# Attention of a macaron block, batch by batch: where values and late scores stand in TensorE's order

## The chip, the cores and the metric

The kernel runs on one core of a Trainium2 chip. The metric is the device time of one execution in microseconds (us), lower is better. TensorE is called PE here, VectorE DVE, ScalarE ACT, GpSimd POOL and SyncE SP, as in the profile.

## What is computed

Sixteen sequences of 256 tokens with 256 channels go through a block of three parts: half a feed-forward, an attention, half a feed-forward, all float32, with a layer norm ahead of each. Each feed-forward has 32 routed experts (4 per token) and a shared one. The attention has 16 query heads and 8 key heads of 32 channels, rotary positions, a soft cap, and a causal mask:

```python
x = x + 0.5 * ffn(layernorm(x))
x = x + attention(layernorm(x))
x = x + 0.5 * ffn(layernorm(x))

# attention, b a sequence, h a query head
att = einsum('bhqd,bhkd->bhqk', q, k) * scale
att = 50.0 * tanh(att / 50.0)
att = where(causal, att, -inf)
y = einsum('bhqk,bhkd->bhqd', softmax(att), v)
```

## The kernel before

**Stages.** The 32 tiles of 128 tokens form eight groups (`NG`) of four tiles, that is of two batches (sequences). The first feed-forward runs first, then the attention over all groups, then the second feed-forward. Work of the shared expert is cut into steps (L382 `shared`: six steps of gate products `pg`, four of output products `po`), which `Fill` hands out wherever PE would otherwise wait: `EXPERT_FILL` says how many us of it stand beside each expert, `SPARE` how many beside the units of the attention. `fill` is the shared expert of the first feed-forward, `fill2` that of the second.

**Order.** PE's order is written by hand throughout. From L734 on that holds for DVE, ACT and POOL too: each of these runs its instructions in the order in which the Python code issues them. Several activities are generators that are advanced by a step now and then, so that their instructions stand between those of others:

- `project(pool, g)` (L478) makes queries, keys and values of group g: reads the sums of the experts (a DMA on SP), adds them on POOL, takes the statistics (`moments`, four pairs of bn_stats and bn_aggr on DVE), normalises on ACT, transposes (`pta`), then eight pieces of products, six `pq` and two `pv`. For a `pq` piece, `turned` (L509) has a shuffle and a product on DVE and a product and a sum on POOL behind two matmuls.
- `route(1, g, rows)` (L232) prepares the second feed-forward's routing of group g: `moments`, then `xr` (four scalings on DVE, L250), two pairs of transposes `pt` with their copies on ACT, the logits `pl` on PE with four copies and reductions on DVE, an Exp on ACT, and a tail of some fourteen small DVE instructions (L299 to L316) ahead of a DMA to `xtab`.

In the loop of the attention `mine` is the projection of the group behind the present one, `ahead` that of the group behind that.

**A unit of the attention.** A unit is a group, one of its two batches and one of two chunks m of four key heads (eight query heads). `scores` (L549) treats the unit's two key tiles one after the other: the first against all 256 queries (matmuls `sc` of 512 columns), the second against the later 128 (256 columns). Each of four matmuls uses 32 rows of the array, `lhsT=kT[r, m, ...]` with `r` one of four strips of 32 partitions, and writes a PSUM bank of its own. Two PSUM tiles of two banks, `big` with two buffers, hold them; `pg` uses the same two buffers. Tanh and Exp follow on ACT, half by half (L568, L571), and POOL cuts the diagonal (L573).

`values` (L586) has five or so groups of four matmuls, each of which writes 32 of the 128 output rows: the softmax's denominators `den`, by a product with ones, and the sums `y`. Its last group is a product of ones with `plate`, which `late_sums` (L580) has DVE add from both key tiles' later queries; units without it sum the wider tile instead. Then DVE turns and inverts the denominators and scales (L610 to L617). `project_out` (L620, `poa`) ends a batch.

**The loop before** (L778) goes over units k. It issues `late_sums` of unit k-1, the first key tile's scores of unit k, `poa` of a finished batch, pieces of `mine` (by `PROJECT_PIECES`), the second key tile's scores of unit k, the values of unit k-1, then steps of routing, spare work and projection. Most value groups thus come right behind the narrow scores.

Of the kernel before, what the change touches and what calls it, by code (L numbers as in the profile page):

```python
# [9 lines left out]
F32 = mybir.dt.float32  # L10
BF16 = mybir.dt.bfloat16
I32 = mybir.dt.int32
AF = mybir.ActivationFunctionType
# [27 lines left out]

ROUTE_FILL, SLOT_FILL, FIRST_FILL, EXPERT_FILL, SUM_FILL, PROJECT_FILL = 3.0, 1.7, 6.0, (2.15, 2.3), 17.0, 1.5
LAST_FILL = 8.0
MASK_FILL, ROW_FILL = 4.0, 3.2
WARM = (9, 3)
AHEAD = 3
SPARE = (0.0, 0.0, 2.0, 3.0)
LAST = 4 * (NG - 1)  # L50
PROJECT_PIECES = ((2, 1), (0, 2), (2, 1), (0, 0))


_COLS = {}
# [39 lines left out]
def macaron_kernel(ctx: ExitStack, tc: tile.TileContext, X, Wq, Wk, Wv, Wo, w_norm, w_router, w_gate, w_up,  # L94
# [451 lines left out]
                    )  # L546
                    yield 1.75

    def scores(pool, u, qT, kT):  # L549

        _, b, m = u
        t0 = b * T
        made = []
        for k0, w in ((0, T), (P, P)):
            dst = pool.tile([P, 4, 2, w], F32, name=f"p{w}", bufs=2)
            sc = [big.tile([P, 2, 2 * T], F32, tag="big", name="sc") for _ in range(2)]
            for i in range(4):
                r = slice(HD * i, HD * (i + 1))  # L560
                nc.tensor.matmul(  # L561
                    sc[i // 2][:, i % 2, 0 : 2 * w].rearrange("p (s t) -> p s t", s=2),
                    lhsT=kT[r, m, t0 + k0 : t0 + k0 + P], rhs=qT[r, m, :, t0 + T - w : t0 + T],
                    start=True, stop=True,
                )
            parts = [dst[:, 2 * h : 2 * h + 2].rearrange("p j s t -> p j (s t)") for h in range(2)]
            for h in range(2):
                nc.scalar.activation(parts[h], sc[h][:, :, 0 : 2 * w], AF.Tanh, scale=QK_SCALE / SOFTCAP)  # L568
            for h in range(2):

                nc.scalar.activation(parts[h], parts[h], AF.Exp, scale=SOFTCAP)  # L571
                diag = dst[:, 2 * h : 2 * h + 2, :, 0:P].rearrange("p j s t -> p (j s) t")
                nc.gpsimd.affine_select(  # L573
                    out=diag, in_=diag, compare_op=ALU.is_ge, fill=0.0,
                    base=0, pattern=[[0, 4], [1, P]], channel_multiplier=-1,
                )
            made.append(dst)
            yield made

    def late_sums(pool, pa, pb):  # L580

        dst = pool.tile([P, 4, 2, P], F32, name="plate", bufs=1)
        nc.vector.tensor_add(dst, pa[:, :, :, P:T], pb)
        return dst

    def values(pool, u, v, pa, pb, pc, yT):  # L586

        _, b, m = u  # L590
        y = ps1.tile([P, 2, T], F32, tag="aux", name="y")
        den = ps1.tile([P, 2, T], F32, tag="aux", name="den")
        late = slice(P, T)
        va, vb = [[v[:, 2 * b + j, 4 * m + i, :] for i in range(4)] for j in range(2)]
        products = [
            (y, slice(0, T), va, pa, True, False),
            (y, late, vb, pb, False, True),
        ]
        if pc is None:
            products = [(den, slice(0, T), [ones] * 4, pa, True, False)] + products  # L600
            products += [(den, late, [ones] * 4, pb, False, True)]
        else:
            products = [(den, slice(0, P), [ones] * 4, pa[:, :, :, 0:P], True, True)] + products
            products += [(den, late, [ones] * 4, pc, True, True)]
        for dst, at, w, p, start, stop in products:
            for i in range(4):
                nc.tensor.matmul(dst[HD * i : HD * (i + 1), :, at], lhsT=w[i], rhs=p[:, i], start=start, stop=stop)  # L607
# [12 lines left out]
    def project_out(g, b, yT):  # L620
        for qh in range(2):
            t = g * GT + 2 * b + qh
            po = ps1.tile([P, C], F32, tag="mm", name="poa")
            for c in range(4):
                nc.tensor.matmul(  # L625
                    po, lhsT=yT[:, c // 2, c % 2, qh * P : (qh + 1) * P], rhs=wo[:, c // 2, c % 2, :],
                    start=(c == 0), stop=(c == 3),
                )
            nc.vector.tensor_add(x[:, t, :], po, x[:, t, :])
# [138 lines left out]
            late.append(i)  # L768

    fill2 = Fill(sh, end)  # L770
    units = [(g, b, m) for g in range(NG) for b in range(2) for m in range(2)]
    with tc.tile_pool(name="attn", bufs=1, reuse_waits="tile") as pool:
        probs, outs, routing = {}, {}, {}

        def spare_time(us):
            (fill if fill.done < NG else fill2).take(us)

        for k in range(len(units) + 2):  # L778
            g, j = divmod(k, 4)
            u = units[k] if k < len(units) else None  # L780
            mine, ahead = projects.get(g + 1), projects.get(g + 2)

            def unit_values():
                if 1 <= k <= len(units):
                    d = units[k - 1]
                    if d[2] == 0:
                        outs[d[:2]] = pool.tile([P, 2, 2, T], F32, name="yT")
                    values(pool, d, made[d[0]][2], *probs.pop(d), outs[d[:2]])

            if 1 <= k <= len(units):
                d = units[k - 1]
                probs[d].append(late_sums(pool, *probs[d]) if 1 < k <= LAST else None)
            if u:
                parts = scores(pool, u, *made[g][:2])
                next(parts)
            if k >= 2 and units[k - 2][2] == 1:
                d = units[k - 2][:2]
                project_out(*d, outs.pop(d))  # L800

            before, behind = PROJECT_PIECES[j] if k != 1 else PROJECT_PIECES[j][::-1]
            advance(mine, before)
            if k == LAST:
                fill2.step()
            if mine is None and j % 2 == 0:
                unit_values()
            if u:
                probs[u] = next(parts)

            if j == 0:
                advance(routing.get(g - 2))
            if j == 2:
                advance(routing.get(g - 2))
            if mine is not None or j % 2:
                unit_values()


            if j == 3 and k > LAST:
                advance(routing.get(g - 1))  # L820
                advance(routing.get(g - 2))
            if j == 3 and k < LAST:
                advance(ahead)

            if k == LAST - 2:
                fill2.gates()
            elif k == LAST + 4:
                fill2.step()
            elif LAST - 2 < k < LAST + 3:
                if k != LAST + 1:  # L830
                    fill2.step()
            elif not LAST - 5 <= k < LAST - 2:
                spare_time(SPARE[j])
            if j == 3 and k < LAST:
                advance(routing.get(g - 1))
                advance(routing.get(g - 2))
            advance(mine, behind)
            if j == 1 and g >= 1:
                routing[g - 1] = route(1, g - 1, rows)
                next(routing[g - 1])  # L840
                advance(routing.get(g - 2))
                fill2.ready = max(g - 1, 0)
            if j == 2:
                advance(routing.get(g - 1))
                advance(ahead)
            if j == 0:
                advance(routing.get(g - 2))

            fill.finish(min(g + 3, NG))
            if j == 3:  # L850
                advance(ahead)
            elif j < 2:
                advance(ahead)
            if j == 3 and g + 3 < NG:
                projects[g + 3] = project(pp, g + 3)
                next(projects[g + 3])
# [45 lines left out]
```

## Time and profile before

| | |
|---|---|
| median of 3 runs | 1051.61 us (1050.84 to 1052.44) |
| the profiled execution | 1051.13 us |
| its span, first to last instruction | 1049.4 us |
| mean granted PE clock over the span | 0.999 |
| PE busy from 800 to 1020 us (second experts) | 215.32 of 220 us |
| DVE busy in the attention, 378 to 755 us | 283.99 of 377 us |
| ACT busy there | 243.88 us |
| POOL busy there | 256.92 us |

A row of the groups reads: line, engine, operation, output and inputs, shapes, count, busy us and mean ns of one. A float32 matmul stands as two passes in the trace, so `x8` of scores are four matmuls. A row of the timeline reads: start in us, length in us, the same names, count, and in brackets the engine's idle time before it and who ended that. Since matmuls overlap at their ends, a group's own cost is read from its start to the start of the next. A row of windows reads: the window, its length, busy us (and instructions) of PE, PE's weight loads, DVE, ACT and POOL, the granted PE clock, the DMA engines' share and GB/s.

### The profile page before, as it was taken

The numbers are of one execution on the slowest core, as the hardware profiler recorded it, in microseconds if no ns is written. First come the engines' busy times: TensorE is split into PE (matmuls) and PEld (weight loads), VectorE is DVE, ScalarE is ACT, GpSimd is POOL, SyncE is SP. The second block draws the span as 40 slices with busy tenths as digits, with TensorE's granted clock in tenths as the row PEclk, the third lists the DMA queues.
The fourth block names the chain that finished last, engine by engine and source line by source line (L and its number), as shares of the span: only waits on it lengthen the run. The fifth ranks groups of instructions, "written<-read, shape, count | busy, mean of one in ns | idle before, by whom it ended". The sixth has DMA issues, their size and how long they took to land.

```text
span 1049.4 us, 15591 instructions
## 1 busy us (share of the span) xinstructions
PE 1024.0 (98%) x5432; PEld 647.1 (62%) x5432; DVE 631.7 (60%) x1684; ACT 400.0 (38%) x761; POOL 495.9 (47%) x548
## 2 busy tenths in 40 slices
PE   9999999999999999999999999999999999999998
PEld 5656656876866455545555555555566576867665
DVE  4964674445353446787878869775756644454453
ACT  3442111222221247675757567667310122222201
POOL 4410102455553379688677767753100245555441
PEclk9999999999999999999999999999999999999999
DMA  9731802788872100000101010000300167777563
GB/s 286 213 120 46 248 6 59 166 167 171 174 164 33 45 22 1 21 21 1 44 1 44 2 43 4 20 23 2 108 23 1 34 133 168 169 167 160 100 202 133
DMA packets 137869, 92.97 MB, mean 89 GB/s; under 512 B 80512, under 2 KB 135104, under 8 KB 137792
## 3 DMA queue, kind: packets, MB, share of 16 engines
q1 hardware_dynamic: 125504, 74.16, 25.6%
q0 software_dynamic: 12288, 17.83, 10.1%
q8 instruction: 43, 0.70, 0.3%
q14 instruction: 34, 0.28, 0.1%
HBM read 60.99 MB, written 30.97 MB: 88 GB/s over the span
## 4 chain that ended last, share of the span: by engine, by line
PE 84%; DVE 7%; POOL 2%; issue 2%; DMA 2%; ACT 1%; POOLq 0%; DVEq 0%; ACTq 0%
PE pg L399 24%; PE po L411 14%; PE pge L446 8%; PE pq L512 7%; PE poe L459 5%; PE poa L625 5%; PE sc L561 5%; PE y L607 3%; PE den L607 3%; PE pv L540 3%; PE pl L283 2%; PE pte L438 1%; DVE xr L250 1%; DVE st L221 1%; PE pa L369 1%
## 5 line engine op out<-in xcount | busy, mean ns | idle before, releaser
L399 PE MATMUL pg<-xnT,sw 128*128 128x512 f32 x704 | 318.5, 597 | 2.0 <-DVE act L405 2.0
L399 PEld LDWEIGHTS pg<-xnT,sw 128*128 128x128 f32 x704 | 130.0, 190 | 138.3 <-issue 130.2
L462 POOL DMA_INDIRECT acc<-y,idx x64 | 101.4, 1584 | 183.8 <-DVE y L461 65.4
L411 PE MATMUL po<-swd,act 128*128 128x256 f32 x768 | 179.3, 383 | 3.9 <-DVE x L415 1.3
L403 ACT ACTIVATE act<-pg 128x512 f32<-128x512 f32 x96 | 57.2, 596 | 288.3 <-PE pg L399 280.5
L411 PEld LDWEIGHTS po<-swd,act 128*128 128x128 f32 x768 | 142.9, 190 | 35.0 <-issue 9.8
L404 DVE SCALAR_TENSOR_TENSOR act<-act,pg 128x512 f32<-128x512 f32 x96 | 65.7, 684 | 152.4 <-ACT act L403 131.1
L568 ACT ACTIVATE p<-sc 128x512 f32<-128x512 f32 (+1 forms) x128 | 97.0, 809 | 81.6 <-PE sc L561 81.2
L422 POOL DMA_INDIRECT xg<-xtab,idx x64 | 68.0, 1062 | 75.4 <-DVE idx L377 56.5
L446 PE MATMUL pge<-xgT,wgu 128*112 128x128 f32 (+1 forms) x768 | 95.9, 275 | 7.7 <-issue 5.7
L571 ACT ACTIVATE p<-p 128x512 f32<-128x512 f32 (+1 forms) x128 | 101.0, 845 | 0.0
L573 POOL TENSOR_SCALAR_AFFINE_SELECT p<-p 128x512 f32<-128x512 f32 x128 | 82.6, 673 | 37.5 <-ACT p L571 36.0
L446 PEld LDWEIGHTS pge<-xgT,wgu 128*112 128x112 f32 (+1 forms) x768 | 88.6, 182 | 11.4 <-issue 11.4
L415 DVE SCALAR_TENSOR_TENSOR x<-po,sg,x 128x256 f32<-128x256 f32 x64 | 30.9, 482 | 72.4 <-PE po L411 70.7
L441 ACT ACTIVATE xgT<-pte,wnorm 128x128 f32<-128x128 f32 x128 | 39.9, 365 | 74.7 <-PE pte L438 65.4
L405 DVE TENSOR_TENSOR act<-act,pg 128x512 f32<-128x512 f32 x96 | 65.7, 684 | 2.3
L459 PE MATMUL poe<-wd,sie 112*128 112x256 f32 x256 | 65.9, 379 | 0.1
L520 POOL TENSOR_TENSOR qs<-qs,kc 128x512 f32<-128x512 f32 x48 | 61.5, 1281 | 9.2 <-DVE qs L515 9.2
L561 PE MATMUL sc<-qT,kT 32*128 32x256 f32 (+1 forms) x512 | 63.5, 533 | 0.4 <-DVE act L405 0.4
L512 PE MATMUL pq<-hT,wq 128*128 128x512 f32 x128 | 60.9, 599 | 0.0
L625 PE MATMUL poa<-wo,yT 128*128 128x256 f32 x256 | 59.7, 386 | 1.2 <-DVE qT L519 1.2
L452 DVE SCALAR_TENSOR_TENSOR sie<-sie,pge 112x256 f32<-112x256 f32 x64 | 26.9, 420 | 53.1 <-ACT sie L451 40.9
(109 smaller groups left out, 1362.1 us busy)
## 6 DMA issues: line engine op xcount, KB each, us to landing
xtab<-xr SPq DMA_DIRECT2D x16, 576.0 KB
acc<-zero SPq DMA_DIRECT2D x2, 4224.0 KB
a<-acc SPq DMA_DIRECT2D x16, 512.0 KB
wgu<-in_L_ffn_w_gate SPq DMA_DIRECT2D x64, 112.0 KB
wgu<-in_L_ffn_w_up SPq DMA_DIRECT2D x64, 112.0 KB
wd<-in_L_ffn_w_down SPq DMA_DIRECT2D x64, 112.0 KB
wgu<-in_L_ffn_w_gate SPq DMA_DIRECT2D x64, 64.0 KB
wgu<-in_L_ffn_w_up SPq DMA_DIRECT2D x64, 64.0 KB
```

What stands on the lines that cost most here:

```text
L399: nc.tensor.matmul(pg[:, s, :], lhsT=sw[:, c, w0 : w0 + P], rhs=xnT[:, c, cols], start=(c == 0), stop=(c == 1))
L411: nc.tensor.matmul(po, lhsT=act[:, k, t * P : (t + 1) * P], rhs=swd[:, k, :], start=(k == 0), stop=(k == len(FC) - 1),)
L422: nc.gpsimd.indirect_dma_start(out=xg, out_offset=None, in_=xtab[n], in_offset=bass.IndirectOffsetOnAxis(ap=idx[:, e : e + 1], axis=0), bo ...
L446: nc.tensor.matmul(pg[:fw, n_, :], lhsT=wgu[:, c, w0 : w0 + fw], rhs=xgT[:, c, :], start=(c == 0), stop=(c == 1))
L459: nc.tensor.matmul(po, lhsT=si[:, k, :], rhs=wd[:, k, :], start=(k == 0), stop=(k == 1))
L462: nc.gpsimd.indirect_dma_start(out=acc[n], out_offset=bass.IndirectOffsetOnAxis(ap=idx[:, e : e + 1], axis=0), in_=y, in_offset=None, boun ...
L512: nc.tensor.matmul(pq, lhsT=weights[:, c, :], rhs=hT[:, c, :], start=(c == 0), stop=(c == 1))
L561: nc.tensor.matmul(sc[i // 2][:, i % 2, 0 : 2 * w].rearrange("p (s t) -> p s t", s=2), lhsT=kT[r, m, t0 + k0 : t0 + k0 + P], rhs=qT[r, m, ...
L568: nc.scalar.activation(parts[h], sc[h][:, :, 0 : 2 * w], AF.Tanh, scale=QK_SCALE / SOFTCAP)
L571: nc.scalar.activation(parts[h], parts[h], AF.Exp, scale=SOFTCAP)
L573: nc.gpsimd.affine_select(out=diag, in_=diag, compare_op=ALU.is_ge, fill=0.0, base=0, pattern=[[0, 4], [1, P]], channel_multiplier=-1,)
L625: nc.tensor.matmul(po, lhsT=yT[:, c // 2, c % 2, qh * P : (qh + 1) * P], rhs=wo[:, c // 2, c % 2, :], start=(c == 0), stop=(c == 3),)
```

## The change

The loop goes over batches instead of units. Each step n has two halves, one for each chunk: `late_sums` and values of batch n-1's chunk, then at once the first key tile's scores of batch n's chunk, then a piece of projection (`between`). The second key tile's scores of both chunks are made together, in one block of eight matmuls whose two chunks share PSUM banks, and one pair of Tanh, Exp and diagonal cut each. Routing, spare work and projection are put at new places around these, and two amounts of fill change. `late_sums` is left out for six units in place of five.

```diff
-ROUTE_FILL, SLOT_FILL, FIRST_FILL, EXPERT_FILL, SUM_FILL, PROJECT_FILL = 3.0, 1.7, 6.0, (2.15, 2.3), 17.0, 1.5
+ROUTE_FILL, SLOT_FILL, FIRST_FILL, EXPERT_FILL, SUM_FILL, PROJECT_FILL = 3.0, 1.7, 6.0, (2.05, 2.3), 17.0, 1.5
...
-SPARE = (0.0, 0.0, 2.0, 3.0)
-LAST = 4 * (NG - 1)
-PROJECT_PIECES = ((2, 1), (0, 2), (2, 1), (0, 0))
+
+SPARE, FIRST_SPARE, LAST_SPARE = 4.0, 2.6, 6.0
...
+    def exponentials(dst, sc):
...
+        parts = [dst[:, 2 * h : 2 * h + 2] for h in range(2)]
+        flat = [p.rearrange("p i m s t -> p i (m s t)") for p in parts]
+        for h in range(2):
+            nc.scalar.activation(flat[h], sc[h], AF.Tanh, scale=QK_SCALE / SOFTCAP)
+        for h in range(2):
+
+            nc.scalar.activation(flat[h], flat[h], AF.Exp, scale=SOFTCAP)
+            diag = parts[h][..., 0:P].rearrange("p i m s t -> p (i m s) t")
+            nc.gpsimd.affine_select(
...
+    def scores(pool, b, chunks, qT, kT, k0):
...
+        t0, w = b * T, T - k0
+        dst = pool.tile([P, 4, len(chunks), 2, w], F32, name=f"p{w}", bufs=3 - len(chunks))
+        sc = [big.tile([P, 2, 2 * T], F32, tag="big", name="sc") for _ in range(2)]
+        for n_, m in enumerate(chunks):
             for i in range(4):
                 r = slice(HD * i, HD * (i + 1))
                 nc.tensor.matmul(
...
+                    sc[i // 2][:, i % 2, n_ * 2 * w : (n_ + 1) * 2 * w].rearrange("p (s t) -> p s t", s=2),
+                    lhsT=kT[r, m, t0 + k0 : t0 + k0 + P], rhs=qT[r, m, :, t0 + k0 : t0 + T],
                     start=True, stop=True,
                 )
...
+        exponentials(dst, sc)
+        return [dst[:, :, n_] for n_ in range(len(chunks))]
...
+        for n in range(2 * NG + 1):
+            g, b = divmod(n, 2)
+            past = divmod(n - 1, 2)
             mine, ahead = projects.get(g + 1), projects.get(g + 2)
...
+            def between():
+
+                if mine is None:
+                    fill2.step()
+                else:
+                    advance(mine)
+
+            def unit_values(m):
+                if n:
+                    if m == 0:
+                        outs[past] = pool.tile([P, 2, 2, T], F32, name="yT")
+                    pa, pb = early.pop((*past, m)), later[past][m]
+
+                    pc = late_sums(pool, pa, pb) if 1 < n < 2 * NG - 1 else None
+                    values(pool, (*past, m), made[past[0]][2], pa, pb, pc, outs[past])
+
+
+
+            unit_values(0)
+            if g < NG:
+                early[g, b, 0] = scores(pool, b, [0], *made[g][:2], 0)[0]
+            between()
+
+            if b == 0:
                 advance(routing.get(g - 2))
+            else:
+                advance(ahead)
+            unit_values(1)
+            if g < NG:
+                early[g, b, 1] = scores(pool, b, [1], *made[g][:2], 0)[0]
+            if n < 2 * NG - 1:
+                between()
+            if b == 0:
+                advance(ahead)
+            else:
+                advance(routing.get(g - 1))
+            if n == 0:
+                advance(mine, 2)
+            elif g < NG:
+                project_out(*past, outs.pop(past))
+            if g < NG:
+                later[g, b] = scores(pool, b, [0, 1], *made[g][:2], P)
+            if b == 0:
                 advance(routing.get(g - 2))
+                advance(mine, 1 if n == 0 else 2)
+                if g < 2:
+                    spare_time(FIRST_SPARE)
+                elif g == NG - 1:
+                    fill2.step()
+                elif g == NG:
+                    fill2.step()
+                    project_out(*past, outs.pop(past))
+                advance(routing.get(g - 2))
+                advance(ahead)
+                if g >= 1:
+                    routing[g - 1] = route(1, g - 1, rows)
+                    next(routing[g - 1])
+                    fill2.ready = max(g - 1, 0)
+            else:
+                advance(routing.get(g - 2))
                 advance(routing.get(g - 1))
+                advance(mine, 2)
+                if g < NG - 2:
+                    spare_time(FIRST_SPARE if g == 0 else SPARE)
+                elif g == NG - 2:
+                    fill2.gates()
+                else:
+                    fill2.take(LAST_SPARE)
+                advance(ahead, 2)
                 advance(routing.get(g - 2))
...
+                if g + 3 < NG:
+                    projects[g + 3] = project(pp, g + 3)
+                    next(projects[g + 3])
             fill.finish(min(g + 3, NG))
```

More of the change, by code (lines that the diff above doesn't have):

```diff
@@ L547, in project @@
                     yield 1.75
[L549 to L558, printed above, removed]
+    def exponentials(dst, sc):
[7 more added lines that the diff above has]
+            nc.gpsimd.affine_select(
+                out=diag, in_=diag, compare_op=ALU.is_ge, fill=0.0,
+                base=0, pattern=[[0, diag.shape[1]], [1, P]], channel_multiplier=-1,
+            )
+    def scores(pool, b, chunks, qT, kT, k0):
[3 more added lines that the diff above has]
+        for n_, m in enumerate(chunks):
             for i in range(4):
@@ L561, in scores @@
                 nc.tensor.matmul(
-                    sc[i // 2][:, i % 2, 0 : 2 * w].rearrange("p (s t) -> p s t", s=2),
-                    lhsT=kT[r, m, t0 + k0 : t0 + k0 + P], rhs=qT[r, m, :, t0 + T - w : t0 + T],
+                    sc[i // 2][:, i % 2, n_ * 2 * w : (n_ + 1) * 2 * w].rearrange("p (s t) -> p s t", s=2),
+                    lhsT=kT[r, m, t0 + k0 : t0 + k0 + P], rhs=qT[r, m, :, t0 + k0 : t0 + T],
                     start=True, stop=True,
                 )
[L566 to L578, printed above, removed]
+        exponentials(dst, sc)
+        return [dst[:, :, n_] for n_ in range(len(chunks))]
     def late_sums(pool, pa, pb):
@@ L770, in macaron_kernel @@
     fill2 = Fill(sh, end)
-    units = [(g, b, m) for g in range(NG) for b in range(2) for m in range(2)]
     with tc.tile_pool(name="attn", bufs=1, reuse_waits="tile") as pool:
-        probs, outs, routing = {}, {}, {}
+        early, later, outs, routing = {}, {}, {}, {}
         def spare_time(us):
             (fill if fill.done < NG else fill2).take(us)
-        for k in range(len(units) + 2):
-            g, j = divmod(k, 4)
-            u = units[k] if k < len(units) else None
+        for n in range(2 * NG + 1):
+            g, b = divmod(n, 2)
+            past = divmod(n - 1, 2)
@@ L781, in macaron_kernel @@
             mine, ahead = projects.get(g + 1), projects.get(g + 2)
[L783 to L809, printed above, removed]
@@ L811, in macaron_kernel @@
-            if j == 0:
-                advance(routing.get(g - 2))
-            if j == 2:
-                advance(routing.get(g - 2))
-            if mine is not None or j % 2:
-                unit_values()
-            if j == 3 and k > LAST:
-                advance(routing.get(g - 1))
-                advance(routing.get(g - 2))
[L822 to L847, printed above, removed]
@@ L849, in macaron_kernel @@
-            fill.finish(min(g + 3, NG))
[L850 to L856, printed above, removed]
+            def between():
[10 more added lines that the diff above has]
+                    values(pool, (*past, m), made[past[0]][2], pa, pb, pc, outs[past])
```

## The prediction

> **What bounds the kernel now.** First the busy shares, then the stretch of the attention (378 to 755 us), then who makes TensorE wait there.
>
> ```profile
> PE 1024.0 (98%) x5432; PEld 647.1 (62%) x5432; DVE 631.7 (60%) x1684; ACT 400.0 (38%) x761; POOL 495.9 (47%) x548
> ```
> ```profile
> 378.00:755.00 377.00, 372.56 (x2443) 201.50 (x2441) 283.99 (x667) 243.88 (x374) 256.92 (x313) 1.00 0.07 22
> ```
> ```profile
> PE poa L625 <- DVE qT L519: 1.2, 1, 1.2
> PE den L607 <- DVE plate L583: 0.9, 2, 0.6
> ```
>
> TensorE (PE) has work for 372.6 of 377 us at the full clock, with hardly any DMA, and waits a few us in all. So a us less of PE's stream is a us of the end, and so is a us in which PE waits. What is in the stream besides arithmetic stands in the starts of PE's groups:
>
> ```profile
> 485.58 1.98 PE L512 MATMUL pq<-hT,wk 128*128 128x512 f32 x4
> 487.40 1.88 PE L512 MATMUL pq<-hT,wq 128*128 128x512 f32 x4
> 489.21 0.71 PE L561 MATMUL sc<-qT,kT 32*128 32x256 f32 x8
> 489.86 0.64 PE L607 MATMUL den<-p,ones 128*32 128x256 f32 x8
> 490.31 1.47 PE L607 MATMUL y<-p,v 128*32 128x512 f32 x16
> 491.60 0.61 PE L607 MATMUL den<-plate,ones 128*32 128x256 f32 x8
> 492.15 3.70 PE L399 MATMUL pg<-xnT,sw 128*128 128x512 f32 x8
> ```
>
> Read from start to start. A 512-wide pass streams in 0.43 us, a 256-wide one in 0.216. Scores (S, 32-row tiles) and values (V, 32-column tiles) run four at a time, so eight 256-wide score matmuls should take 0.43; they take 0.65. The difference sits at each change of the array's shape: about 0.10 on the last instruction before it and 0.10 on the first after it (0.02 where V begins). With F for full-size work: F to S 0.20, S to F 0.21, S to V 0.13, V to S 0.22, V to F 0.22, F to V 0.12.
>
> **Part 1, fewer changes of shape.** I counted them in the order of the built programs, attention alone. Before: 61, 34, 30, 3, 29, 2 in the sequence above, 30.4 us. After: 18, 48, 0, 30, 2, 32, 24.4 us. Joining the two chunks in one block assumes that the second pair of passes costs only its streaming; the row-tiled `pa` passes of the slots stage, several of which follow each other, show only the first of them longer (0.215 against 0.111). One more unit goes without late sums, and its wide sum of ones costs 0.4. Gain 5.6.
>
> **Part 2, waits that go.** Six score blocks of before ran in two halves, as a PSUM pair was not free (the page's waits on DVE act at scores, 0.4 us, are part of it): 1.54 or 2.4 in place of 1.07, together 4.6. With the 0.9 on plate and 1.2 on poa shown, 6.7; none of it has to vanish, so 0 to 6.7. A value block of 2.2 us now stands ahead of the first scores, which gives the pairs their time, so I take 6.7.
>
> **Part 3, the wait that comes.** The value block needs `plate`, the sum that VectorE makes in `late_sums`, for its last product. Before, `late_sums` stood at the start of a unit and a score block, a `poa` or `pq` and another score block lay between. Now it is issued just ahead of the value block, which reaches plate after 0.43+0.02+0.86+0.43 = 1.74 us. VectorE works strictly in program order (its trace has the order of the build). This is before, with the step of routing and the statistics ahead of plate:
>
> ```profile
> 533.84 0.42 DVE L221 BATCH_NORM_STATS2 st<-x 128x6 f32<-128x256 f32 x1
> ...
> 535.97 0.26 DVE L287 COPY lg<-pl 128x132 f32<-128x132 f32 x1
> ...
> 536.87 0.42 DVE L221 BATCH_NORM_STATS2 st<-x 128x6 f32<-128x256 f32 x1
> ...
> 539.00 1.19 DVE L583 TENSOR_TENSOR plate<-p,p 128x1024 f32<-128x1024 f32 x1
> 540.12 0.01 DVE L515 LOAD_MASK_SELECT qs<-pq  x1
> ```
>
> From 533.84 to 540.12, 6.28 us: four statistics 2.13, the four copies and reductions of logits 0.90, four more statistics 2.13, plate 1.12. PE reached its den of plate at 541.92: hidden.
>
> The new loop's step n issues the scores of batch n and the values of batch n-1, in two value blocks. First block, odd n. The build has on PE pl, then the values at once; and VectorE: the four logit steps, which wait for pl, all eight statistics, plate. The copy starts about 0.13 after the value block does; plate is there at 0.13+6.28+0.06 = 6.47, PE wants it at 1.74: 4.7 us. Four steps so (5, 7, 9, 11); step 3 has no logits (4.4), step 13 four statistics (2.6). Sum 25.8.
>
> First block, even n. On PE pg, two pta (0.98 with the shape), values; on VectorE the two steps of that pg, the tail of routing, plate:
>
> ```profile
> 606.73 0.69 DVE L404 SCALAR_TENSOR_TENSOR act<-act,pg 128x512 f32<-128x512 f32 x1 [2.15 <-ACT act L403]
> 607.45 0.69 DVE L405 TENSOR_TENSOR act<-act,pg 128x512 f32<-128x512 f32 x1
> 608.05 0.28 DVE L299 TENSOR_REDUCE tot<-ex 128x4 f32<-128x128 f32 x1
> ...
> 610.86 1.21 DVE L583 TENSOR_TENSOR plate<-p,p 128x1024 f32<-128x1024 f32 x1
> ```
>
> Counted from the end of pg: ScalarE's Tanh and two VectorE steps 2.24, tail 2.81, plate 1.2: 6.3, wanted at 0.98+1.74 = 2.7. That is 3.55 for n = 6, 8, 10, 12; step 14 has no pta and waits 4.45; step 4 has no pg and waits 0.3. Sum 19.0.
>
> Second block. Behind the first one VectorE turns the sums (L610 to L615, 2.48, begun 0.68 after the last product starts), then serves the pq between (1.24) and only then adds plate: 6.05 against PE's 5.28, so 0.77 in six even steps; with a pv between (copy 0.61) about 0.17 in six odd ones. Sum 5.6.
>
> ScalarE: the merged block puts two Tanh and two Exp of 1024 (4.2) ahead of the copies of pt (0.94), and pl needs these 4.0 after the block's end: 5.2 against 4.0, 1.2 five times, 6.2. VectorE again: `xr` (four, 4.1 with GpSimd busy beside it) precedes the adds of poa, so pt's PSUM tile is late by 0.7 to 1.3 in six odd steps, 5.4. Step 16 has pg and a tail between its two value blocks, 2.0.
>
> All waits 25.8+19.0+5.6+6.2+5.4+2.0 = 64.0. Behind a waiting value product on PE stands everything else, the next scores first, so nothing covers these. The merging saves ScalarE some 12 us of fixed cost and leaves POOL's selected elements as they are, neither on the path. Steps of routing and projection that move take their DMAs on SP along: xtab is written and acc read some us later or earlier, with 7% of the DMA engines busy; zero. EXPERT_FILL moves 34 x 0.1 = 3.4 us of PE's fill from the experts to later, the same PE work: 0, or 0.4 for one more uncovered expert.
>
> **The clock.** No wait of before is long enough to show what a 4.7 us gap does to TensorE, except the last:
>
> ```profile
> 1040.00:1049.00 9.00, 5.80 (x27) 4.75 (x26) 2.72 (x6) 0.00 (x0) 0.00 (x0) 0.95 0.16 54
> ```
>
> PE's last matmul ends at 1045.8; a mean clock of 0.95 over 9 us is 0.9 us at half clock, so it fell about 2.35 us after the last matmul. The Trainium skill (TensorE: Matmul & The Clock Gate, "What's actually happening") puts it at a full free-running idle window of some 3.4 us, and the same time of work to come back. By the row, some eight of the waits above (all the long odd ones, two thirds of the 3.55 ones) drop the clock; by the page about two (a 4.7 us gap holds a whole window in 4 of 10 cases). Coming back took the first matmuls from 1.19 to 6.9 us at half speed; in a busy stretch I estimate 2.5 us lost each (a window and a half at half speed, from the page's length). Eight give 20, two 5. I take the five gaps well over both bounds, 12.5, less 1 of the small waits it hides: 11.5.
>
> Sum: 1051.1 - 5.6 - 6.7 + 64.0 + 11.5 = 1114.3 against the profiled execution; the median of the runs is 0.5 above that, so 1115.
>
> **Rivals.** (a) The shape changes decide: if plate were ready within 1.74 us at every value block, PE's stream would only get shorter, 1051.6 - 5.6 - 6.7 = 1039, or 1045 if only the shapes give. It needs new waits of under 12 us in total; for it speaks that the work of PE is what counts and is cut for certain, against it that the 6.28 us chain is measured and stands in the build behind pl. (b) Only the chain behind pl binds: the tails run in slack of their own, as VectorE is ahead there, and the clock holds. Without 19.0 and 11.5, 1084. For it: the tail's inputs are early; against: it is queued behind pg's two steps. (c) The clock drops in eight waits, 8.5 more, and ScalarE or POOL is late for the merged block by up to 1 us in each of 15 steps: up to 1138. That the build doesn't place values beside scores can be excluded; it has 30 such neighbours in place of 3.
>
> **Chances.** Forecast 0.60, (b) 0.17, (c) 0.13, (a) 0.07, a cancelling mixture around no change 0.03. About 0.2% is what a measurement here tells from no change. The range 1072 to 1138 covers the forecast with its bounds, (b) and most of (c).
>
> **What would show it.** In the profile after: PE waiting on DVE plate for 40 to 55 us, the longest waits in odd steps near 4.7, others on ACT xnT at pl; a granted clock under 1 within the attention; 16 merged score blocks, each 1.07 from start to start. If plate waits total under 10 us, the reasoning about VectorE's order is wrong; if they are as said and the clock stays 1, the time is about 1103.

## The result, and the profile after

The changed kernel takes 1153.26 us (median of 6 runs, 1151.33 to 1160.0) against 1051.69 before (6 runs): a ratio of 1.0964, 95% interval 1.0942 to 1.0986. The forecast of 1115 had the sign right and the size too small: +63 in place of +101.6, with the time outside the range.

From the profile after, the busy shares and the granted clock over the span:

```profile
PE 1049.1 (91%) x5432; PEld 653.5 (57%) x5432; DVE 622.8 (54%) x1683; ACT 391.2 (34%) x697; POOL 491.5 (43%) x516
...
PEclk9999999999999999989899999998999999999989
```

PE has the same 5432 matmuls. It lost seven points of its share, and the clock, nearly full before, dips from the middle on. The attention, and two neighbouring stretches of 10 us inside it:

```profile
382.50:835.50 453.00, 382.28 (x2389) 198.92 (x2392) 264.46 (x619) 231.87 (x302) 245.72 (x270) 0.94 0.05 16
562.00:572.00 10.00, 5.39 (x30) 2.34 (x23) 7.11 (x20) 1.83 (x3) 5.55 (x11) 0.66 0.00 0
572.00:582.00 10.00, 9.73 (x68) 5.28 (x67) 7.86 (x13) 7.78 (x11) 4.01 (x5) 1.00 0.01 2
```

The first row is the whole stage: 453 us, PE idle for 71 of them, at a clock of 0.94. The second row is a value block that waits for plate: half idle, the clock at 0.66, while the row after it is full. So the loss comes in single places. Who makes PE wait, whole kernel:

```profile
PE den L609 <- DVE plate L585: 49.5, 18, 4.6
PE pq L511 <- DVE qT L518: 8.4, 6, 1.4
PE pv L539 <- DVE qT L518: 7.5, 5, 1.5
...
PE po L410 <- DVE x L414: 5.0, 3, 4.4
```

A row gives the idle time in total, the number of waits and the longest. The first row was 0.9 us before and the last 1.3; the two between are new. Inside one step (n = 7) PE's timeline shows the wait, and DVE's shows what it is made of:

```profile
560.49 0.64 PE L609 MATMUL den<-p,ones 128*32 128x256 f32 x8
560.95 1.47 PE L609 MATMUL y<-p,v 128*32 128x512 f32 x16
567.03 1.08 PE L609 MATMUL den<-plate,ones 128*32 128x256 f32 x8 [4.61 <-DVE plate L585]
```
```profile
560.60 0.30 DVE L286 COPY lg<-pl 128x132 f32<-128x132 f32 x1 [1.01 <-PE pl L282]
...
561.53 0.42 DVE L220 BATCH_NORM_STATS2 st<-x 128x6 f32<-128x256 f32 x1
...
565.78 1.19 DVE L585 TENSOR_TENSOR plate<-p,p 128x1024 f32<-128x1024 f32 x1
```

DVE begins the logits 0.11 us after PE begins the value block, works without a pause through logits and eight statistics (561.53 to 565.78) and only then adds plate; PE reads it 6.54 us after the block began. Before, the same chain of 6.28 us ran under score and projection work. The matmuls on plate show 1.08 in place of 0.64: they ran at half clock.

**Where the 101 us are.** I summed PE from start to start of its passes, each against what its width streams, and put each excess down to a wait, to a change of shape or to half clock. (A wait counted so is some 0.2 us longer than the idle time in a row of the profile.) Between the two profiled executions (1051.13 and 1152.32):

| us | before | after |
|---|---|---|
| attention: streaming | 321.8 | 329.1 |
| attention: waits | 4.6 | 78.2 |
| attention: half clock | 0 | 21.8 |
| attention: changes of shape | 28.3 | 23.3 |
| all other stages: streaming | 663.4 | 654.0 |
| all other stages: waits | 24.7 | 34.2 |
| all other stages: half clock | 0 | 4.4 |
| all other stages: changes of shape | 1.4 | 0.3 |

The clock rows can be had in a second way: the trace has 61.4 us at half clock, 8.6 of them in gaps where PE has nothing to lose; half of the rest is 26.4.

For the waits and the clock of the other stages the forecast had no term. Some 9.4 us of the shared expert's matmuls stand in the attention now (44.7 in place of 35.3) and not around it: 2.5 came from ahead of the attention and 6.8 from behind the last routed expert. Yet the stages around it did not get shorter. At the kernel's end that is plain:

```profile
1111.68 5.49 PE L410 MATMUL po<-swd,act 128*128 128x256 f32 x12 [4.36 <-DVE x L414]
```

PE waits 4.36 us for DVE's `x`, which stands in DVE's queue behind an addition (L767) that waits 8.14 us for the read-back of the experts' sums. There are 40.8 us of shared-expert work after the last routed expert in place of 47.7; the end takes 53.1 us in place of 52.7.

### The profile page after: what moved, and what is told of

The parts are those of the page before. It is cut to its first block, busy times and chain, and to the rows that moved or that the text cites. A ratio compares the mean times of both kernels' runs of the same rounds, so it can differ in the third digit from the quotient of the medians.

```text
span 1150.6 us, 15482 instructions
## 1 busy us (share of the span) xinstructions
PE 1049.1 (91%) x5432; PEld 653.5 (57%) x5432; DVE 622.8 (54%) x1683; ACT 391.2 (34%) x697; POOL 491.5 (43%) x516
## 4 chain that ended last, share of the span: by engine, by line
PE 77%; DVE 15%; issue 2%; ACT 2%; DMA 2%; POOL 2%; DVEq 0%; POOLq 0%; ACTq 0%
PE pg L398 24%; PE po L410 12%; PE pq L511 8%; PE pge L445 7%; PE sc L574 5%; PE poa L627 5%; PE poe L458 4%; DVE plate L585 3%; PE pv L539 3%; PE den L609 2%; PE pl L282 2%; DVE st L220 2%; DVE act L403 1%; DVE qs L514 1%; PE pte L437 1%
## 5 line engine op out<-in xcount | busy, mean ns | idle before, releaser
L410 PE MATMUL po<-swd,act 128*128 128x256 f32 x768 | 184.0, 391 | 10.0 <-DVE x L414 5.0
L410 PEld LDWEIGHTS po<-swd,act 128*128 128x128 f32 x768 | 146.3, 195 | 42.1 <-issue 11.9
L554 ACT ACTIVATE p<-sc 128x1024 f32<-128x1024 f32 x96 | 93.0, 1021 | 186.0 <-PE sc L574 179.6
L559 POOL TENSOR_SCALAR_AFFINE_SELECT p<-p 128x512 f32<-128x512 f32 (+1 forms) x96 | 80.3, 845 | 155.5 <-ACT p L557 137.7
L557 ACT ACTIVATE p<-p 128x1024 f32<-128x1024 f32 x96 | 96.2, 1058 | 0.0
L445 PEld LDWEIGHTS pge<-xgT,wgu 128*112 128x112 f32 (+1 forms) x768 | 88.6, 182 | 10.6 <-issue 10.6
L519 POOL TENSOR_TENSOR qs<-qs,kc 128x512 f32<-128x512 f32 x48 | 64.9, 1353 | 12.5 <-DVE qs L514 12.5
L511 PE MATMUL pq<-hT,wq 128*128 128x512 f32 x128 | 61.4, 606 | 8.4 <-DVE qT L518 8.4
L609 PE MATMUL den<-plate,ones 128*32 128x256 f32 x208 | 18.8, 438 | 50.0 <-DVE plate L585 49.5
```

What stands on the lines that cost most here:

```text
L410: nc.tensor.matmul(po, lhsT=act[:, k, t * P : (t + 1) * P], rhs=swd[:, k, :], start=(k == 0), stop=(k == len(FC) - 1),)
L445: nc.tensor.matmul(pg[:fw, n_, :], lhsT=wgu[:, c, w0 : w0 + fw], rhs=xgT[:, c, :], start=(c == 0), stop=(c == 1))
L511: nc.tensor.matmul(pq, lhsT=weights[:, c, :], rhs=hT[:, c, :], start=(c == 0), stop=(c == 1))
L554: nc.scalar.activation(flat[h], sc[h], AF.Tanh, scale=QK_SCALE / SOFTCAP)
L557: nc.scalar.activation(flat[h], flat[h], AF.Exp, scale=SOFTCAP)
L559: nc.gpsimd.affine_select(out=diag, in_=diag, compare_op=ALU.is_ge, fill=0.0, base=0, pattern=[[0, diag.shape[1]], [1, P]], channel_multip ...
```

## Experiments

The theory: DVE's order makes plate late, and each long wait also costs clock. The rivals: the merged score block on ACT is the main cause; late issue of the sum is enough by itself; or the changed neighbours on PE are worth nothing at all. Runs e1 to e8 and e11 are one execution each. The six of the changed kernel spread over 8.7 us, so a difference of a few us between two of them says little.

**e1: no unit has late sums.** All 32 units take the wider product of ones; plate is not made.

```diff
-                    pc = late_sums(pool, pa, pb) if 1 < n < 2 * NG - 1 else None
+                    pc = None
```

> The changed kernel without late sums at all: every value block takes its denominators from the two key tiles directly, which costs PE 0.43 us in each of 26 units, 11 us. Theory O (VectorE's program order ahead of plate makes PE wait, and the waits drop the clock): the 54 us of waits on plate go and most of the 26 us of half clock with them, 1152 - 54 - 24 + 11 = 1085. Rival P (ScalarE and POOL are late with the merged block, plate is only where it shows): PE waits as long at the products of p instead, 1150 to 1165.

1095.85 (the kernel before beside it: 1053.08), 11 above the forecast. The 54.4 us of plate waits are gone and half clock falls from 26.3 to 5.7, for 10.6 us more streaming; some 7 us of other waits came up in the place of the longer ones. So plate with its clock is more than half of the loss. Of the 43 us that are left, 10.6 are the price of this edit; the other 32 do not hang on plate's sum. That ACT is the main cause would have kept the time at 1150 or more.

**e2: PE is kept busy while it waits.** The first value blocks repeat the product of ones for the later queries, which plate's product then overwrites.

```diff
+            products += [(den, late, [ones] * 4, pa[:, :, :, 0:P], True, True)] * again
             products += [(den, late, [ones] * 4, pc, True, True)]
...
+                    again = {3: 9, 5: 9, 7: 9, 9: 9, 11: 9, 13: 4, 6: 6, 8: 6, 10: 6, 12: 6, 14: 9}
```

> The changed kernel with the wait of the first value block filled: the product of ones with p of the early half is made 4 to 9 times more into the place that plate's product then overwrites (0.43 us each, less than the wait in each case), so PE has work while VectorE is on its way to plate. Theory O: plate comes at the same time, but the clock stays whole, so only the 26 us of half clock go (of them some 3 us at the end of the kernel stay): about 1129. Rival C (the clock drops for another reason than these waits): 1152. Rival P as O.

1136.74, where 1129 was expected. Windows of this kernel, over most of the attention:

```profile
380.00:780.00 400.00, 366.98 (x2830) 197.88 (x2829) 246.93 (x565) 213.11 (x275) 237.56 (x254) 1.00 0.05 16
```

The clock is back at 1.00. The useless products cost 39 us, the plate waits shrink by 36.5, so the rest of the gain is clock: half clock falls by 19.3. This isolates what the waits do to the clock. It was 11.5 in the forecast of the change.

**e3: the first chunk's sum is issued at the end of the step before.**

```diff
+            def sum_ahead():
+                if 0 < n < 2 * NG - 2:
+                    plates[g, b] = late_sums(pool, early[g, b, 0], later[g, b][0])
...
                 advance(mine, 2)
+                sum_ahead()
```

> The changed kernel with only the first chunk's late sum issued earlier: at the end of a step, behind the pieces of projection that follow the merged scores, ahead of VectorE's logits, statistics and routing tail. The second chunk's stays. Theory O: the waits of the first blocks (about 46 of the 54 us) and nearly all of the half clock go, 1152 - 46 - 24 = 1082; those of the second blocks (6 to 8 us) stay. Rival P: the sum is now early but waits for POOL's cut of the merged block, and PE still waits, 1130 or more.

1118.04, a gain of 34 where some 70 were expected. The plate waits fell to 11.4 and half clock to 8.5, but waits for `yT` (11.7) and `dT` (8.1) came up: the statistics now stand ahead of the turning of the first block's sums, and the second block needs those PSUM tiles. The wait for DVE's `x` at the kernel's end grew too, from 4.4 to 7.4.

**e4: the routing's transposes `pt` away from the merged scores.** They go ahead of them in one half of the steps, behind two projection pieces in the other.

```diff
+            if b == 0:
+                advance(routing.get(g - 2))
             if g < NG:
                 later[g, b] = scores(pool, b, [0, 1], *made[g][:2], P)
...
-                advance(routing.get(g - 1))
                 advance(mine, 2)
+                advance(routing.get(g - 1))
```

> The changed kernel with only routing's transposes pt moved: in the first step of a group ahead of the merged scores, in the second behind the two pieces of projection, so that they don't hold a PSUM buffer while ScalarE works on the merged block. If that is why PE waits 17.6 us at pq and pv: about 1135, and plate's waits unchanged. If those waits are VectorE's lateness from the rest of the step: no change, 1150, the wait at pq as before.

1136.99, near the forecast, but in part by luck (below). The waits for `qT` at pq and pv are gone, which in the changed kernel look like this on PE and on ACT:

```profile
486.97 0.66 PE L266 MATMUL pt<-kc,xr 128*128 128x128 f32 x4
...
490.85 2.00 PE L539 MATMUL pv<-wv,hT 128*128 128x256 f32 x8 [1.50 <-DVE qT L518]
```
```profile
487.14 1.94 ACT L554 ACTIVATE p<-sc 128x1024 f32<-128x1024 f32 x2 [2.67 <-PE sc L574]
...
490.85 0.84 ACT L269 ACTIVATE xnT<-pt,wnorm 128x256 f32<-128x256 f32 x2
```

`pt` and the projection share two PSUM buffers. `pt` holds one from 487 until ACT copies it at 490.85, behind two merged Tanh and two Exp; the projection goes round on the other, and pv waits until DVE has emptied it. The wait's row names DVE; what makes it is ACT, and moving pt ends it. Plate waits meanwhile rose by 9.7 to 64.1, with gaps of 6.1, where no change was expected; and half clock fell by some 7.5, as fewer gaps cost the clock. The two nearly cancel, so what pt's place is worth is the 17.6 us of waits that went, not the 15.3 of the time.

**e5: the kernel before, with the sum issued just ahead of the values.** This is the late issue alone.

```diff
+                    pc = late_sums(pool, pa, pb) if 1 < k <= LAST else None
+                    values(pool, d, made[d[0]][2], pa, pb, pc, outs[d[:2]])
...
-                probs[d].append(late_sums(pool, *probs[d]) if 1 < k <= LAST else None)
```

> The kernel before with one edit: each late sum is issued just ahead of its values, as in the changed kernel, instead of at the start of the unit. Theory O in its sharper form (it counts what VectorE still has to do between its last wait for PE and plate; in this loop the statistics and the routing tail stand a score block and a projection ahead of the values): short waits of 0.2 to 0.5 us, 1055 to 1062. Rival (issuing the sum late is itself the cost): some 50 us of waits on plate, 1100 or more.

1068.46 against 1051.4, above the 1055 to 1062 expected and far below the rival's 1100. In the waits of this kernel:

```profile
PE den L607 <- DVE plate L583: 15.4, 18, 1.7
```

About 0.9 us at each of 18 units and no drop of the clock. In the loop before, the late issue by itself costs some 17 of the 101; in the changed kernel it is the work that stands ahead of the sum on DVE that makes 3.3 to 4.6 of it.

**e6: both sums early and pt moved.** e3 and e4 together, and the second chunk's sum ahead of the first `between`.

```diff
+            if 1 < n < 2 * NG - 1:
+                plates[past] = late_sums(pool, early[(*past, 1)], later[past][1])
             between()
```

> The changed kernel with the first late sum early (as in e3), the second one ahead of the piece of projection between, and pt moved (as in e4). Nothing about the statistics and the tail, which now stand ahead of the first block's reciprocals instead. Theory O: plate's waits under 5 us, those at pq and pv gone, but some 15 to 20 us stay as waits of the second value block for the first one's PSUM (y, den): 1085 to 1095. If waits on VectorE are only about plate: 1065.

1107.11, a miss (1085 to 1095 expected). DVE and PE of this kernel in one step:

```profile
546.99 2.29 DVE L585 TENSOR_TENSOR plate<-p,p 128x1024 f32<-128x1024 f32 x1 [0.85 <-POOL p L559]
...
550.87 0.42 DVE L220 BATCH_NORM_STATS2 st<-x 128x6 f32<-128x256 f32 x1
...
555.11 0.68 DVE L612 STREAM_TRANSPOSE dT<-den 128x512 f32<-128x512 f32 x1
```
```profile
555.85 0.64 PE L609 MATMUL den<-p,ones 128*32 128x256 f32 x8 [2.88 <-DVE dT L612]
```

Plate is early, and the 4.2 us of statistics (550.87 to 555.11) now delay `dT`, which empties the PSUM tile that the second block's den wants. The wait has changed its name and kept its cause.

**e7: the statistics and tails spread as well.** e6, with the routing's statistics begun behind poa's, the projection's moved ahead of the logits, and the tail between the projection pieces and the gate products.

```diff
                 later[g, b] = scores(pool, b, [0, 1], *made[g][:2], P)
...
+                if g < NG:
+                    route_begin()
                 advance(mine, 1 if n == 0 else 2)
                 sum_ahead()
+                advance(ahead)
...
-                advance(routing.get(g - 2))
                 advance(mine, 2)
+                advance(routing.get(g - 2))
```

> As e6, and VectorE's long stretches spread: routing's statistics go behind the adds of poa, the projection's ahead of the logits, the routing tail between the projection's pieces and the spare gate products. Theory O: under 15 us of waits in the attention, almost no half clock there: 1060 to 1072. The end of the kernel still costs some 8 us more than before (a shorter rest of fill). If VectorE's total work is the limit now, waits only move: 1085.

1088.92: 18 better than e6, still 17 above the upper end of what was expected. Plate waits are 12.1 and half clock 12.0; the wait at the end of the kernel is 9.8. The time is near the 1085 of the other reading, that DVE's total work is the limit now. The attention of this kernel speaks against that:

```profile
384.10:770.10 386.00, 368.67 (x2394) 197.17 (x2392) 270.19 (x619) 232.92 (x302) 243.14 (x270) 0.97 0.06 18
```

DVE is busy for 270 of 386 us, 70%. In the kernel before it was busy for 75% (284 of 377), and PE hardly waited.

**e8: e7 with more work left for the end.** Only the fill beside the second routed experts is smaller.

```diff
-... EXPERT_FILL, ... = ... (2.05, 2.3), ...
+... EXPERT_FILL, ... = ... (2.05, 2.1), ...
```

> As e7 with EXPERT_FILL of the second feed-forward 2.1 in place of 2.3, so that some 7 us more of shared work is left for the end, where PE waited 4.4 us at half clock for the sums. Expected 6 to 9 us less than e7. If the end waits for something else: as e7.

1077.15, 11.8 less than e7. The work behind the last routed expert, first in e7, then in e8:

```profile
1030.90:1087.20 56.30, 45.08 (x145) 28.77 (x143) 21.71 (x33) 4.18 (x7) 18.67 (x9) 0.91 0.51 156
1021.25:1075.45 54.20, 48.94 (x161) 29.80 (x159) 24.47 (x37) 5.37 (x9) 18.94 (x9) 1.00 0.53 162
```

With as much shared-expert work there again as before the change, the end takes 54.2 us in place of 56.3 at full clock, and the second experts 153.9 in place of 159.2. The wait at the end falls from 9.8 to 3.8. So the amount of fill left for the end counts, though PE's work is the same in sum. It is worth these 7.4 us, as expected, and not the whole 11.8: the other 4.3 lie ahead of the second experts, where e7 and e8 run the same instructions. There e7 has three drops of the clock in the attention and e8 two.

**e11: e8 with the tail back behind the gate products, and one more output product in step 13.**

```diff
                 advance(mine, 2)
-                advance(routing.get(g - 2))
                 advance(routing.get(g - 1))
...
+                    fill2.take(2.6)
...
                 advance(ahead, 2)
+                advance(routing.get(g - 2))
```

> As e8, with the routing tail back at the end of the step behind the spare gate products (the sum stays ahead of both), and one more output product of the shared expert in step 13. The waits of 1.5 us in even steps become some 0.7, the 4 us one of step 14 goes and its drop of the clock with it: 1066 to 1070. If the tail ahead of the reciprocals costs as much as ahead of plate: 1077 as e8.

1083.7, a miss. Plate fell to 3.0 as meant and the attention became 5 us shorter, but `yT` rose to 8.6, and the extra product was taken from the end, where the wait was 9.8 again. A new wait stands just behind the attention, too:

```profile
779.67 6.12 PE L410 MATMUL po<-swd,act 128*128 128x256 f32 x14 [4.78 <-DVE act L404]
```

It cost the clock as well. In e8 no wait for `act` is longer than 1.7 us; why this one is was not tested.

**e9, e10, e12: the kernel before, with some values beside scores.** The first key tile's scores of the next unit are begun right behind the values of units of place j in the group, so that late sums and all else stay where they were; both chunks' late scores stay apart. In e9 j is 0, 1, 2.

```diff
                 unit_values()
+                if k and j in (0, 1, 2):
+                    begin(k + 1)
...
+            if j == 2 and k < LAST - 2:
+                advance(mine, behind)
+                behind = 0
```

> The kernel before with the changed kernel's first idea alone: in three of four units the first key tile's scores of the next unit come right behind the values (narrow scores, values, wide scores in one run), with late sums, statistics and tail where they were; in the third unit of a group a projection piece goes ahead of the spare gate products. The built order has 41, 35, 29, 23, 9, 3 changes of shape in place of 61, 34, 30, 3, 29, 2: 3.7 us less by the prices read off the trace. If the price list holds and VectorE's order is what hurt: 1046 to 1049. If placing values beside wide scores is itself bad for the waits: slower than 1052.

1055.82, ratio 1.0038 (1.0025 to 1.005), where 1046 to 1049 was expected; so its other branch (slower than 1052) came true. What fewer changes of shape save is more than lost in waits.

```profile
PE poa L625 <- DVE qT L519: 5.8, 6, 1.1
```

It was 1.2 before. `poa` waits six times for DVE's `qT`, whose projection piece had moved up next to it; plate's waits rose from 0.9 to 2.6.

e10 has j in (0, 1, 2, 3).

> As e9 in all four units, where in the last unit of a group the spare gate products follow the wide scores closely and need the PSUM pairs that Tanh still reads. 5.1 us less of shape changes, but up to 7 waits of 1 to 2 us for the pair: 1047 to 1056. If the pair is free in time: 1046.

1081.72, ratio 1.0277 (1.0258 to 1.0296), a miss: the PSUM pair that was feared costs little. In its waits:

```profile
PE pta L503 <- ACT hT L504: 11.1, 4, 3.4
```

Scores begun a unit early put their Tanh and Exp ahead of the copies of `hT` on ACT. Gaps of 3.4 and 3.9 us cost the clock as well (9.7).

e12 has j in (1, 2).

> As e9, but only behind the values of the second and third unit of a group: there no poa follows at once, which in e9 waited 1.06 us a group for a PSUM buffer that pq held (6.8 us in all). 14 neighbours of values and wide scores are added to those of before, 0.19 us each by the price list: 2.7 us less shape cost and about 2 us of waits on plate that come closer. If both hold: 1049 to 1051. If the waits cost as much as the changes of shape save: 1052, no difference that can be measured.

1050.53 (22 runs) against 1051.82 (27 runs beside them), ratio 0.9984 (0.9975 to 0.9993). Changes of shape fall from 29.7 to 27.3, and waits rise by 2.0. Four of the six score blocks that ran in two halves before, for want of a free PSUM pair, run in one here, which gives another 1.9 (the sum of these blocks falls from 38.8 to 36.9). It is the fastest of all the kernels here, by under 0.2%.

## Why the prediction was right and wrong

The mechanism was right and the sum 38 us short. The terms that failed are the clock (14.7 short), the waits outside the attention (9.5, put at nothing), ACT's merged block (7.7) and the credit (5.9). The fourth row of the forecast below is its credit of 6.7 and the 2.0 of step 16.

| term of the sum, us | forecast | measured |
|---|---|---|
| changes of shape | -5.6 | -6.1 |
| DVE's order ahead of plate | +50.4 | +53.1 |
| behind ACT's merged block (pl, pt) | +11.6 | +19.3 |
| other waits of the attention | -4.7 | +1.2 |
| half clock | +11.5 | +26.2 |
| waits outside the attention | 0 | +9.5 |
| streaming | 0 | -2.1 |
| sum | +63.2 | +101.1 |

**Right: the sequence on DVE.** The waits at plate by kind, forecast and then measured idle time: first blocks of odd steps 25.8 and 24.8 (4.7 each and 4.6; step 3 4.4 and 3.9; step 13 2.6 and 2.5), of even steps 19.0 and 17.7 (3.55 and 3.33; step 14 4.45 and 4.42), second blocks 5.6 and 7.0 (0.77 in even steps and 0.9 to 1.7). Counting what DVE has issued between its last wait for PE and the sum, at durations from the trace before, was good to a few per cent for the long waits. The merged score blocks take 1.07 from start to start (485.90 to 486.97), as said, and shapes give about what was said. That rules out rival (a), and also (b), which had no waits in even steps; of the rivals (c), with more drops of the clock, came nearest, though the time lies beyond its 1138 too and its waits for the merged block came at other places. (Its sum for shapes alone in (a) is 1046, not 1045.)

**Wrong in size: the clock, "I take the five gaps well over both bounds, 12.5".** This term missed most, 11.5 for 26.2. The forecast's own list has six waits of 4.4 us and more, not five. The row of before, a drop 2.35 us after the last matmul, said some eight; I halved it towards the full window of the page that the forecast cites. All eleven gaps at plate of 2.49 us and more dropped the clock, as did the 4.36 at the end and one pair of 1.68 and 0.71: 13 drops, 2.0 us of loss each. The 2.5 per drop was nearly right; the count failed.

Which gaps drop it can be read from the traces. All 13 drops begin on one grid of 3.41 us: those at 448.62, 499.82 and 537.37 lie 15 and 11 steps apart. They lasted 3.41 or 6.83 us, one or two of the free-running windows that the Trainium skill gives (TensorE: Matmul & The Clock Gate, "What's actually happening"). But a window need not be idle throughout. Two neighbouring stretches of the grid in the changed kernel (n = 7), then two in e4:

```profile
561.26:564.67 3.41, 1.16 (x16) 0.26 (x8) 3.17 (x14) 0.00 (x0) 0.75 (x2) 1.00 0.00 0
564.67:568.08 3.41, 1.05 (x12) 0.24 (x12) 2.24 (x6) 0.00 (x0) 2.96 (x5) 0.50 0.00 0
```
```profile
586.56:589.98 3.42, 1.52 (x22) 0.39 (x12) 3.17 (x20) 0.38 (x1) 1.78 (x3) 1.00 0.53 160
589.98:593.39 3.41, 1.85 (x17) 0.69 (x18) 2.55 (x6) 0.11 (x1) 0.00 (x0) 1.00 0.48 171
```

In the first pair PE is idle for 2.25 of the 3.41 us, and the next stretch runs at half clock. In e4 PE waits for 3.46 us (588.08 to 591.53), but a border of the grid cuts the gap, each side keeps PE idle for 1.9 us or less, and the clock holds. In the changed kernel every drop follows a stretch in which PE was idle for 2.05 us or more, and no stretch with 1.97 or less was followed by one. Over all 14 traces, behind the first 30 us, all 43 stretches with 2.0 us or more of idle time dropped the clock, none with under 1.2 did, and of 98 between 13 did; what decides there stays open. The 2.35 us of before were the idle part of such a stretch, and not the least length of a gap.

**Wrong in size: ACT's merged block.** 11.6 was placed at pl and at pt's own tile. Those show 1.7 and nothing; the price was paid at the projection pieces that share PSUM with pt, eleven times at 1.6, 17.6 in all. The cause was the one I gave, 4 us of Tanh and Exp ahead of the copies of pt; I had not asked who else uses the buffer that pt holds meanwhile. e4 shows it.

**Wrong: "the same PE work: 0, or 0.4 for one more uncovered expert".** PE's work stayed the same in sum (streaming -2.1), but the conclusion did not follow. 9.4 us of fill moved and not only the 3.4 counted, and the stages outside the attention got 9.5 of waits and 4.4 of half clock. At the end, which gave up 6.8, PE waits for the chain of DMA and DVE shown above (some 4.5 of waits and 3.0 of clock); e8 shows for the spread variant that fill left there gives time back, 7.4. The stage between the attention and the second experts gave up nothing and still took 4.8 more, with these waits in it:

```profile
PE po L410 <- DVE act L404: 2.5, 3, 1.7
```

What made them, and the rest ahead of the attention, was not tested.

**Wrong: the credit of 6.7.** The waits it named did go; small others, such as y behind POOL's cut (1.7), came in their place.

**The idea itself.** Values beside scores need not cost: e12 has them behind two units of four, with late sums left early, and is slightly faster. Behind three and four units (e9, e10) the time rises, by waits at poa and for `hT`. What costs is what the new order does to the queues of DVE and ACT and to the PSUM buffers; that the full order could be had without such waits is not shown. e3, e6 and e11 each moved something and met the next in the queue; e8, the best of them, is still 26 us above the kernel before. Open is whether its rest can be removed, and where the 2.1 of streaming went: the passes are the same in number.

## What to carry to other kernels

Before a consumer on PE is moved, write down the in-order queue of the engine that makes its operand from that engine's last wait for PE on; if it is longer than PE's way there, the difference is the wait, and moving only the operand hands the wait to the next in the queue. Where a wait appears in a stream that ran at full clock, ask how much of one 3.41 us stretch it can leave idle: here a wait of 4 us always left 2 us in one of two neighbours and cost about 2 us more, one of 2 to 4 us did so only where it fell well. Ask of every PSUM tile kept longer who else takes turns with it. Fill that is moved is not neutral though PE's work is: where it leaves, the stage may stay as long as before.

## What was not expected of the hardware

A gap in PE's work of 2.5 us was enough for half clock over the next 3.4 or 6.8 us, while some of 3.46 us cost none: what counted was the idle share of a stretch of a fixed grid. The drop can come after the wait is over (n = 9: the wait ends at 628.74, the clock falls at 629.53), on matmuls that wait for nothing. And adding the two halves of plate (the same `TENSOR_TENSOR` of 1024 columns) took 1.19 us in one place and 2.15 to 2.29 in others; what it ran beside was not varied here.
